# Edge sums of a graph stack: counted on VectorE in layer 2 instead of multiplied on TensorE in layer 1

## The chip, the cores and the metric

The kernel runs on one core of one Trainium2 chip. The core has five engines that run side by side, each with its own queue of instructions that it takes strictly in order: TensorE (PE in the profile; its weight loads are listed as PEld), VectorE (DVE), ScalarE (ACT), GpSimd (POOL) and SyncE (SP). Sixteen DMA engines move data; transfers are issued from the queues of SP, ACT and POOL. Engines wait for each other and for transfers by semaphores. The metric is the time of one execution on the device in microseconds.

## The reference, cut to what matters

A 4096 x 256 matrix `x` passes through four layers that share one 4096 x 4096 adjacency matrix `adj` of zeros and ones. Each layer adds its input and normalizes its rows.

```python
# layer 0
deg = sum(adj, axis=1); agg = adj @ x / max(deg, 1)
x = layernorm(x + relu(concat([x, agg]) @ W + b))
# layer 1, two steps; R = (adj + I) with rows scaled to sum 1
for n in range(2):
    A = top_p_attention(Xa, W1, W2, W3)     # softmax, the largest up to mass 0.9
    Xf = R @ Xf
    Xa = A @ Xa
    Z = Z + Xf @ U1[n].T + Xa @ U2[n].T
x = layernorm(x + layernorm(X + Z) * ln_g + ln_b)
# layer 2
neighbor_edge = einsum('ij,ji->i', adj, adj)[:, None]
x = layernorm(x + concat([x, adj @ x, neighbor_edge]) @ weight + bias)
# layer 3
x = layernorm(x + relu(normalized(adj + I) @ x @ W + b))
```

The change concerns `neighbor_edge`, the edge sum: for node i the number of nodes j with both `adj[i, j]` and `adj[j, i]` set. It is one number per row and is used in layer 2 alone. In the kernel it is the array `nef`, one column per tile of 128 rows.

## The kernel before, in words

**Tiles.** N = 4096 rows make 32 tiles of 128 (P). `adj` comes in twice as blocks of 128 x 128: `adjt` holds the transposed blocks of a row of tiles, `adjn` the blocks that stand opposite them. Both are f32 in memory; a transfer from POOL's queue turns them into 8-bit floats (F8) on the way in. Matrix products with `adj` use the 8-bit block, widened by ScalarE, as weights, and a right side of 512 columns: the upper bits of the operand and the rest (`split`, `load_halves`), so that two passes give f32 precision.

**Layer 0** (`l0_main`, up to about 350 us): for each tile `adjt` is loaded as `a8`, written back to memory as 8-bit `adj8_d`, widened in four pieces and multiplied. `column_counts` (L287) finds the row degrees on VectorE: the bytes of `a8` are added in pairs as 16-bit numbers, halving the width each time, with one shift to keep the bytes from running over; one 16-bit TensorE product with a column of ones adds the 128 partitions (`l0_degrees`, L304).

**Layer 1** (`run_step`, L941) is two steps over 32 tiles in a software pipeline. For index i it makes the logits of tile i + 2 (`logits_chunk`), searches the largest of tile i + 1 (`peak_groups`, `exp_rows`, `tops`, `pick`), and multiplies tile i (`pieces`, L720), in eight groups g. In step 0 a tile keeps 16 entries a row: POOL gathers the 16 sets of rows from memory (`gather`, L666, eight slots `G`), VectorE makes diagonal weights `dg`, TensorE multiplies (L758). Rows that need more are put off: `flag` (L579) counts them with two products of one column (L589, L590: `ones_sq`, `before`) and a scatter from POOL writes them to a list in memory (L603).

Beside this runs R @ Xf, one tile per index (`neighbours`, L674): SP loads two groups of 8-bit blocks from `adj8_d` (L678), ScalarE widens them (L680), TensorE multiplies (L683), `r_end` (L700) scales and stores. In step 0 alone the same blocks, still 8-bit, are multiplied with those of `adjn` (L693) into a bank `nef_ps`; `r_end` takes its diagonal on VectorE (L707) as the edge sum. The blocks of `adjn` are loaded from POOL's queue (L689) as halves of a tile, 256 KB each after conversion, into two buffers `b8`. While the edge products use the PSUM bank `nef`, the products of R use `acc` alone; from the end of step 0 on (`nef_done`) they take both in turn.

**Layer 2** (from about 2723 to 3002 us) and **layer 3** (to 3238 us): `piece` (L1102) loads a quarter of a tile's 8-bit blocks on SP and widens it on ScalarE, `main` multiplies 32 blocks into one of two banks, `l2_end` (L1126) adds the residual (`xi`), the bias, the part made ahead (`u`, from `zu_d`) and `w2e_sb * nef`, and normalizes; its power of -1/2 (L197) is POOL's. `l2_y` (L1144) makes layer 3's operand. Layer 2 begins after a loop that every engine enters together (`left_over`, L921), by loading the first pieces and the right side `zh` from `zu_d` (L1110).

**What sets the order.** The program text gives data dependences and a priority; a scheduler lays each engine's instructions out in one fixed order when the kernel is built, by costs and due times of its own. A buffer of a pool is used again when its last reader is done; that wait stands in the queue of whoever writes the buffer next, and what follows in that queue waits behind it.

Of the kernel before, what the change touches and what calls it, by code (L numbers as in the profile page):

```python
# [54 lines left out]
def gnn_stack(ctx, tc, x, adjt, adjn, w0, b0, w1, w2t, w3t, u1t, u2t, ln_g, ln_b, w2, b2, w3, b3, out):  # L55
# [44 lines left out]
    nc.vector.memset(ones_col, 1.0)  # L100
    mhalf = const.tile([P, 1], F32, name="mhalf")
# [18 lines left out]
    adj8_d = [dram.tile([P, NT, P], F8, name=f"adj8_{it}_d") for it in range(NT)]  # L120
    h_d = dram.tile([N + P, D], F32, name="h_d")
# [97 lines left out]

    with tc.tile_pool(name="l0", bufs=1) as l0, tc.tile_pool(name="l0w", bufs=2) as l0w:  # L220
# [28 lines left out]
        ones_bf = l0.tile([P, 1], BF16, name="ones_bf")  # L249
        nc.vector.memset(ones_bf, 1.0)  # L250
# [20 lines left out]
        def l0_main(it):  # L271
            acc = ps_acc.tile([P, 512], F32, tag=("acc", "nef")[it % 2], name="acc")

            a8 = l0.tile([P, NT, P], F8, tag="in", name="a8", bufs=SLOTS_IN)
            for s in (slice(0, NT // 2), slice(NT // 2, NT)):
                nc.gpsimd.dma_start(a8[:, s, :], adjt[it, :, s, :])
                nc.sync.dma_start(adj8_d[it][:, s, :], a8[:, s, :])

            def piece(it, c):
                a = l0w.tile([P, JP, P], F32R, tag="adjt", name="a", bufs=4)  # L280
                nc.scalar.copy(a, a8[:, c * JP : (c + 1) * JP, :])
                return a

            adj_matmul(l0w, acc, it, lambda jt: y0h[:, jt, :], piece)
            return acc, column_counts(a8)

        def column_counts(a8):  # L287

            pairs = a8.bitcast(U16).rearrange("p j i -> p (j i)")
            W = NT * P // 4  # L290
            s = l0w.tile([P, W], U16, tag="sums", name="sums", bufs=1)
            nc.vector.tensor_add(s, pairs[:, :W], pairs[:, W:])
            W //= 2
            nc.vector.tensor_add(s[:, :W], s[:, :W], s[:, W : 2 * W])
            words = s[:, :W].bitcast(I32)
            nc.vector.tensor_scalar(words, words, 3, None, op0=ALU.logical_shift_right)
            while W > P // 2:
                W //= 2
                nc.vector.tensor_add(s[:, :W], s[:, :W], s[:, W : 2 * W])
            counts = l0w.tile([P, P], BF16, tag="counts", name="counts")  # L300
            nc.vector.tensor_copy(counts, s[:, :W].bitcast(U8))
            return counts
# [49 lines left out]
    with tc.tile_pool(name="l1", bufs=1, reuse_waits="tile") as l1:  # L352

        cur = {"late": False, "n": 0, "nef_done": False}
# [4 lines left out]
        ones_sq = l1.tile([P, P], F32, name="ones_sq")  # L359
        nc.vector.memset(ones_sq, 1.0)  # L360

        before = l1.tile([P, P], F32, name="before")
# [216 lines left out]
        def flag(st):  # L579
# [9 lines left out]
            nc.tensor.matmul(pb[:, 0:1], ones_sq, st["bad"], start=True, stop=True)  # L589
            nc.tensor.matmul(pb[:, 1:2], before, st["bad"], start=True, stop=True)  # L590
# [83 lines left out]
        def neighbours(n, i, g, acc_r, pn, xf):  # L674

            if g % 2 == 0:
                cur["a8"] = cur["w"].tile([P, 2 * GP, P], F8, tag="adj8", name="adj8", bufs=3)
                nc.sync.dma_start(cur["a8"], adj8_d[i][:, g * GP : (g + 2) * GP, :])  # L678
            a = cur["w"].tile([P, GP, P], F32R, tag="adjq", name="adjq", bufs=2)
            nc.scalar.copy(a, cur["a8"][:, g % 2 * GP : (g % 2 + 1) * GP, :])  # L680
            for j in range(GP):
                jt = g * GP + j
                nc.tensor.matmul(acc_r, a[:, j, :], xf[:, jt, :], start=(jt == 0), stop=False)  # L683
            if g + 1 == NLC:
                nc.tensor.matmul(acc_r, ident_r, xf[:, i, :], start=False, stop=True)
            if pn is not None:
                if g % (NLC // 2) == 0:
                    cur["b8"] = cur["w"].tile([P, NT // 2, P], F8, tag="adjn8", name="adjn8", bufs=2)
                    nc.gpsimd.dma_start(cur["b8"], adjn[i, :, g * GP : g * GP + NT // 2, :])  # L689
                k = g % (NLC // 2) * GP  # L690
                for j in range(GP):
                    jt = g * GP + j
                    nc.tensor.matmul(pn[:, :P], cur["a8"][:, g % 2 * GP + j, :], cur["b8"][:, k + j, :], start=(jt == 0),  # L693
                                     stop=(jt == NT - 1))

        def r_acc(i):

            return ps_acc.tile([P, 512], F32, tag=("acc", "nef")[i % 2 if cur["nef_done"] else 0], name="acc_r", bufs=1)

        def r_end(i, acc_r, pn):  # L700
            xf_new = work.tile([P, D], F32, tag="xf_new", name="xf_new", bufs=1)
            nc.scalar.activation(xf_new, acc_r[:, :D], AF.Copy, scale=rs[:, i : i + 1])
            nc.vector.scalar_tensor_tensor(xf_new, acc_r[:, D:], rs[:, i : i + 1], xf_new, op0=ALU.mult, op1=ALU.add)
            if pn is not None:

                junk = spare_row.bitcast(F32)[:, :P]
                nc.vector.scalar_tensor_tensor(junk, pn[:, :P], 1.0, ident, op0=ALU.mult, op1=ALU.mult,  # L707
                                               accum_out=nef[:, i : i + 1])
            nc.sync.dma_start(rows(xf_d, i), xf_new)

        def r_product(n, i, xf):

            acc_r, pn = r_acc(i), None
            if n == 0:
                pn = ps_acc.tile([P, 512], F32, tag="nef", name="nef_ps", bufs=1)
            for g in range(NLC):
                neighbours(n, i, g, acc_r, pn, xf)
            r_end(i, acc_r, pn)

        def pieces(n, st, nxt, ops, rs_now=()):  # L720
# [10 lines left out]
            if with_r:  # L731
                i, = rs_now
                acc_r, pn = r_acc(i), None
                if n == 0:
                    pn = ps_acc.tile([P, 512], F32, tag="nef", name="nef_ps", bufs=1)
# [12 lines left out]
            for g in range(NLC):  # L748
# [19 lines left out]
                if with_r:  # L768
                    neighbours(n, i, g, acc_r, pn, cur["xf"])
# [11 lines left out]
            if with_r:  # L781
                r_end(i, acc_r, pn)
# [158 lines left out]
        def run_step(n, es):  # L941
# [99 lines left out]
            if n == 0:  # L1041
# [7 lines left out]
                cur["nef_done"] = True  # L1049
# [51 lines left out]
    with tc.tile_pool(name="l23", bufs=1, reuse_waits="tile") as l23:  # L1101
        def piece(it, c):  # L1102
            a8 = l23.tile([P, JP, P], F8, tag="a8", name="a8", bufs=5)
            nc.sync.dma_start(a8, adj8_d[it][:, c * JP : (c + 1) * JP, :])
            a = l23.tile([P, JP, P], F32R, tag="adjt", name="a", bufs=4)
# [3 lines left out]
        ahead = [piece(0, c) for c in range(NJP)]  # L1109
        zh = load_halves(l23.tile([P, 4 * J0 * D], F32, name="scratch"), zu_d[:N, :], nc.sync, slice(0, D))  # L1110
# [5 lines left out]
        yh = [pool.tile([P, NT // 2, 2 * D], F32R, tag="X", name=f"yh{k}") for k, pool in enumerate((xpool, l23))]  # L1116

# [3 lines left out]
        def main(it, halves):  # L1121
            acc = ps_acc.tile([P, 512], F32, tag=("acc", "nef")[it % 2], name="acc")
            adj_matmul(l23, acc, it, halves, lambda it, c: ahead.pop(0) if ahead else piece(it, c))
            return acc

        def l2_end(it, acc):  # L1126
# [7 lines left out]
            nc.vector.tensor_add(xi, xi, b2_sb)  # L1134
            nc.vector.tensor_add(u, u, xi)
# [34 lines left out]
        for it in range(NT):  # L1170
            acc = main(it, lambda jt: zh[:, jt, :])
# [54 lines left out]
```

## Time and profile before

| | us |
|---|---|
| median of 17 runs | 3248.4 |
| lowest and highest | 3228.41, 3255.78 |
| the profiled execution, its own time | 3253.88 |
| its span, first to last instruction | 3252.2 |
| layer 0 and first loads | 0 to about 350 |
| layer 1, step 0 | about 357 to 1250 |
| layer 1, step 1, put-off rows and zu | to about 2710 |
| layer 2 | 2723 to 3002 |
| layer 3 | 3002 to 3238 |

The profile is one execution. Its first part gives busy time by engine; the second cuts the span into 40 slices and shows the busy tenths of each; windows do the same for stretches that one names. Groups of instructions show line, engine, operation, `out<-in`, shapes and count, then the busy time, the mean time of one in ns, and how long the engine stood idle just before them, with what ended that. Successive TensorE instructions overlap, so their mean time is a latency; what one costs is the distance from start to start. Waits list who waited for whom: microseconds in total, times, and the longest.

### The profile page before, as it was taken

How to read it: one execution, taken by the hardware profiler on the slowest of the kernel's cores; microseconds unless marked ns; L12 is line 12 of the kernel's file. 1: busy time of each engine (PE TensorE's matmuls, PEld its weight loads, DVE VectorE, ACT ScalarE, POOL GpSimd, SP SyncE). 2: the span in 40 equal slices, each digit the busy share in tenths (PEclk: the TensorE clock that was granted, in tenths of full speed). 3: DMA queues.
4: the chain of work that ended last, by engine and by line, in shares of the span. 5: the costliest groups of instructions: out<-in, count | busy, mean ns of one | idle time of the engine just before them, and what ended most of it. 6: DMA issues, size and time to landing. Idle time of an engine off the chain costs nothing. (4 is left out here: it accounts for less than half of the span.)

```text
span 3252.2 us, 45754 instructions
## 1 busy us (share of the span) xinstructions
PE 2964.4 (91%) x14376; PEld 2339.7 (72%) x14376; DVE 2291.0 (70%) x7161; ACT 1746.2 (54%) x2906; POOL 789.2 (24%) x915
## 2 busy tenths in 40 slices
PE   7999889999999996799998999999999796999998
PEld 3788667777777774578877777877788554887886
DVE  4566778887787775268988896989799663444444
ACT  3555655665555553365545454645555334666664
POOL 1121256676666664000000001000100100000000
PEclk9999999999999997899999999999999898999999
DMA  9995468777777775230001110011011134333332
GB/s 171 162 174 115 83 117 137 141 141 139 138 139 139 137 135 129 90 91 20 23 25 25 33 38 27 28 35 38 24 36 28 61 127 132 107 110 102 104 109 81
DMA packets 247872, 300.14 MB, mean 92 GB/s; under 512 B 34688, under 2 KB 201536, under 8 KB 247616
## 3 DMA queue, kind: packets, MB, share of 16 engines
q0 software_dynamic: 46576, 104.94, 23.1%
q1 hardware_dynamic: 188800, 180.93, 18.5%
q10 hardware_dynamic: 12240, 11.23, 1.1%
q8 instruction: 116, 1.90, 0.3%
q14 instruction: 140, 1.15, 0.2%
HBM read 331.17 MB, written 66.45 MB: 122 GB/s over the span
## 5 line engine op out<-in xcount | busy, mean ns | idle before, releaser
L683 PE MATMUL acc_r<-xh,adjq 128*128 128x512 f32 x2048 | 610.7, 429 | 25.8 <-ACT adjq L680 14.9
L766 PE MATMUL acc_bank<-xa,at 128*128 128x256 f32 x2304 | 569.3, 388 | 29.9 <-ACT at L744 29.3
L669 POOL DMA_INDIRECT G<-x_d,cols x512 | 498.3, 973 | 290.6 <-PE acc_bank L758 177.6
L680 ACT CAST adjq<-adj 128x512 fp32r<-128x512 fp8e4 x512 | 316.4, 620 | 392.9 <-PE acc_r L683 309.6
L766 PEld LDWEIGHTS acc_bank<-xa,at 128*128 128x128 f32 x2304 | 424.6, 194 | 91.6 <-ACT at L744 40.5
L683 PEld LDWEIGHTS acc_r<-xh,adjq 128*128 128x128 f32 x2048 | 376.9, 191 | 122.0 <-ACT adjq L680 42.5
L197 POOL TENSOR_TENSOR rstd<-ve,mhalf 128x1 f32<-128x1 f32 x168 | 103.1, 614 | 1344.2 <-DVE ve L195 1289.9
L430 DVE MAX8 cand<-e 128x8 f32<-128x256 f32 x1024 | 383.1, 415 | 64.8 <-ACT e L412 63.5
L412 ACT COPY e<-lg 128x512 f32<-128x512 f32 x552 | 319.5, 585 | 196.9 <-PE lg L411 193.1
L411 PE MATMUL lg<-kS,q 128*128 128x512 f32 x1104 | 401.3, 449 | 4.8 <-ACT e L412 4.7
L758 PE MATMUL acc_bank<-G,dg 128*128 128x256 f32 x1024 | 291.5, 401 | 82.7 <-DMA G<-x_d,cols 72.7
L1106 ACT CAST a<-a 128x1024 fp32r<-128x1024 fp8e4 x256 | 267.9, 1048 | 158.7 <-PE acc L173 122.3
L758 PEld LDWEIGHTS acc_bank<-G,dg 128*128 128x128 f32 x1024 | 196.7, 198 | 140.2 <-DMA G<-x_d,cols 85.5
L527 DVE FIND_INDEX8 cols<-top,e 128x8 uint32<-128x4096 f32 x64 | 282.8, 4419 | 0.0
L173 PE MATMUL acc<-xh,a 128*128 128x512 f32 x1024 | 256.3, 403 | 22.3 <-DMA x2i<-x_d 17.8
L173 PE MATMUL acc<-y0h,a 128*128 128x512 f32 x1024 | 253.5, 400 | 0.0
L173 PEld LDWEIGHTS acc<-xh,a 128*128 128x128 f32 x1024 | 191.5, 190 | 66.4 <-ACT xh L149 24.5
L173 PE MATMUL acc<-yh,a 128*128 128x512 f32 x1024 | 233.7, 390 | 0.0
L744 ACT COPY at<-at_ps 128x512 f32<-128x512 f32 x296 | 173.5, 588 | 99.8 <-PE at_ps L741 98.1
L185 ACT COPY xt<-tr 128x256 f32<-128x256 f32 (+1 forms) x268 | 112.0, 425 | 212.9 <-PE tr L183 195.7
L173 PEld LDWEIGHTS acc<-yh,a 128*128 128x128 f32 x1024 | 192.1, 188 | 39.7
L173 PEld LDWEIGHTS acc<-y0h,a 128*128 128x128 f32 x1024 | 187.9, 188 | 42.2 <-issue 0.6
(287 smaller groups left out, 4598.9 us busy)
## 6 DMA issues: line engine op xcount, KB each, us to landing
adj<-adj_d SPq DMA_DIRECT2D x256, 128.0 KB
a<-adj_d SPq DMA_DIRECT2D x256, 128.0 KB
a<-in_adjt POOLq DMA_DIRECT2D x64, 256.0 KB
adj_d<-a SPq DMA_DIRECT2D x64, 256.0 KB
adjn<-in_adjn POOLq DMA_DIRECT2D x64, 256.0 KB
x_d<-x SPq DMA_DIRECT2D x64, 128.0 KB
xf_d<-xf_new SPq DMA_DIRECT2D x64, 128.0 KB
G<-x_d,cols POOLq DMA_INDIRECT x512
```

The costliest lines, as they stand in the source:

```text
L173: nc.tensor.matmul(acc, a[:, j, :], halves(jt), start=(jt == 0), stop=(jt == NT - 1))
L411: nc.tensor.matmul(pl[:, :LC], q[k], kS[:, s], start=(k == 0), stop=(k == 1))
L412: nc.scalar.copy(l[:, s], pl[:, :LC])
L430: nc.vector.max(dst[:, 8 * g : 8 * g + 8], src[:, g * GW : (g + 1) * GW])
L527: nc.vector.max_index(st["at"][:, 8 * r : 8 * r + 8], t8, st["e"][:, :N])
L669: nc.gpsimd.indirect_dma_start(out=g, out_offset=None, in_=x1_d, in_offset=bass.IndirectOffsetOnAxis(ap=st["at"][:, k : k + 1], axis=0))
L680: nc.scalar.copy(a, cur["a8"][:, g % 2 * GP : (g % 2 + 1) * GP, :])
L683: nc.tensor.matmul(acc_r, a[:, j, :], xf[:, jt, :], start=(jt == 0), stop=False)
L744: nc.scalar.copy(at[:, :G, :], ps[:, :G, :])
L758: nc.tensor.matmul(acc_a, dg[:, k % 4, :], st["G"][k], start=(k == 0), stop=(k == KEPT - 1))
L766: nc.tensor.matmul(acc_a, ats[g][:, j, :], cur["xa"][:, jt, :], start=(jt == 0), stop=(jt == NT - 1))
L1106: nc.scalar.copy(a, a8)
```

## The change: what it does

- In step 0 the edge products (L693) and their diagonal sums (L707) go. `neighbours` still loads the `adjn` blocks, and `keep_edges` writes each half from SP to a new tensor in memory, `adjn8_d`. A write is issued when the next half is asked for, so that it stands one half later in program order; `run_step` issues the last one. The products of R use the banks `acc` and `nef` in turn in both steps.
- In layer 2 `edge_row` loads a tile's 512 KB of `adjn8_d` on SP, two tiles ahead into two buffers. For each quarter, `both` takes on VectorE the bitwise and of the two 8-bit copies, as 32-bit words. `edge_count` runs `column_counts` on the result, adds the partitions with one TensorE product, and puts the number into `nef`.
- `column_counts` moves out of layer 0 and takes the pool as an argument; `ones_bf` becomes a constant of the whole kernel.
- Two additions of `l2_end` (`xi + b2`, `u + xi`) move from VectorE to GpSimd.
- `flag` copies `bad` to 16 bits; `ones_sq` and `before` are 16-bit too.
- The scratch of layer 2's start takes the memory of `yh`'s second half.

```diff
@@ neighbours, keep_edges, r_acc, r_end
-            if pn is not None:
-                if g % (NLC // 2) == 0:
-                    cur["b8"] = cur["w"].tile([P, NT // 2, P], F8, tag="adjn8", name="adjn8", bufs=2)
-                    nc.gpsimd.dma_start(cur["b8"], adjn[i, :, g * GP : g * GP + NT // 2, :])
-                k = g % (NLC // 2) * GP
-                for j in range(GP):
-                    jt = g * GP + j
-                    nc.tensor.matmul(pn[:, :P], cur["a8"][:, g % 2 * GP + j, :], cur["b8"][:, k + j, :], start=(jt == 0),
-                                     stop=(jt == NT - 1))
+            if edges and g % (NLC // 2) == 0:
+                half = slice(g * GP, g * GP + NT // 2)
+                t = cur["w"].tile([P, NT // 2, P], F8, tag="adjn8", name="adjn8", bufs=2)
+                nc.gpsimd.dma_start(t, adjn[i, :, half, :])
+                keep_edges(adjn8_d[i][:, half, :], t)
+
+        def keep_edges(dst=None, src=None):
+
+            if "edges" in cur:
+                nc.sync.dma_start(*cur.pop("edges"))
+            if dst is not None:
+                cur["edges"] = dst, src
...
-            return ps_acc.tile([P, 512], F32, tag=("acc", "nef")[i % 2 if cur["nef_done"] else 0], name="acc_r", bufs=1)
+            return ps_acc.tile([P, 512], F32, tag=("acc", "nef")[i % 2], name="acc_r", bufs=1)
...
-            if pn is not None:
-
-                junk = spare_row.bitcast(F32)[:, :P]
-                nc.vector.scalar_tensor_tensor(junk, pn[:, :P], 1.0, ident, op0=ALU.mult, op1=ALU.mult,
-                                               accum_out=nef[:, i : i + 1])
@@ flag
-            nc.tensor.matmul(pb[:, 0:1], ones_sq, st["bad"], start=True, stop=True)
-            nc.tensor.matmul(pb[:, 1:2], before, st["bad"], start=True, stop=True)
+            bad = small("bad16", 1, BF16)
+            nc.vector.tensor_copy(bad, st["bad"])
+            nc.tensor.matmul(pb[:, 0:1], ones_sq, bad, start=True, stop=True)
+            nc.tensor.matmul(pb[:, 1:2], before, bad, start=True, stop=True)
@@ layer 2
+        def edge_row(it):
+
+            b8 = l23.tile([P, NT, P], F8, tag="b8", name="b8", bufs=2)
+            nc.sync.dma_start(b8, adjn8_d[it])
+            return b8
+
+        def both(it, c, a8):
+
+            b = edge_rows[it][:, c * JP : (c + 1) * JP, :].bitcast(I32)
+            nc.vector.tensor_tensor(b, b, a8.bitcast(I32), op=ALU.bitwise_and)
+
+        def edge_count(it):
+
+            counts = column_counts(l23, edge_rows.pop(it))
+            ps = half("acc")
+            nc.tensor.matmul(ps[:, 0:1], counts, ones_bf, start=True, stop=True)
+            n = l23.tile([P, 1], I32, tag="edges", name="edges", bufs=2)
+            nc.vector.tensor_scalar(n, ps[:, 0:1], 1.0 / PER_ONE, None, op0=ALU.mult)
+            nc.vector.tensor_copy(nef[:, it : it + 1], n)
+
+        edge_rows = {0: edge_row(0), 1: edge_row(1)}
+        ahead = [piece(0, c, True) for c in range(NJP)]
+        zh = load_halves(l23.tile([P, NT * D], F32, tag="X", name="scratch"), zu_d[:N, :], nc.sync, slice(0, D))
...
-            nc.vector.tensor_add(xi, xi, b2_sb)
-            nc.vector.tensor_add(u, u, xi)
+            nc.gpsimd.tensor_add(xi, xi, b2_sb)
+            nc.gpsimd.tensor_add(u, u, xi)
...
-            acc = main(it, lambda jt: zh[:, jt, :])
+            acc = main(it, lambda jt: zh[:, jt, :], True)
+            edge_count(it)
+            if it + 2 < NT:
+                edge_rows[it + 2] = edge_row(it + 2)
```

## The prediction

> **What bounds the kernel now.** The page came first: TensorE (PE) is busy in 91% of the span, and its tenths stay at 9 nearly throughout, so a stage's length is PE's work plus the waits left in it. Second, the stages the change touches, by windows. Step 0 of layer 1 runs from about 357 to 1223 us, layer 2 from 2723 to 3002 us.
>
> ```profile
> PE 2964.4 (91%) x14376; PEld 2339.7 (72%) x14376; DVE 2291.0 (70%) x7161; ACT 1746.2 (54%) x2906; POOL 789.2 (24%) x915
> ...
> DMA  9995468777777775230001110011011134333332
> ```
>
> ```profile
> core 0: us, PE busy (x) PEld busy (x) DVE busy (x) ACT busy (x) POOL busy (x), PEclk, DMA share, GB/s
> ...
> 490.00:1222.00 732.00, 678.12 (x3739) 538.00 (x3738) 588.56 (x1737) 432.25 (x834) 486.32 (x512) 0.98 0.77 138
> ...
> 2755.00:3000.00 245.00, 245.00 (x1092) 197.10 (x1092) 106.29 (x316) 158.94 (x231) 15.91 (x29) 1.00 0.35 108
> ```
>
> ```profile
> 357.00:592.00 235.00, 10.98 (x19) 0.94 0.72 126
> 592.00:1223.00 631.00, 27.26 (x45) 0.98 0.77 138
> ```
>
> The last two rows are the edge blocks' loads alone (adjn, 64 of them): 19 are issued before 592 us and 45 after, spread evenly, while the 16 DMA engines are busy 72% and 77% of the time. So step 0 has a second resource that is nearly as full as PE. Layer 2 is PE's alone: 245 of 245 us.
>
> Third, who waits in step 0. PE waits for one thing only, gathered rows, and POOL, which issues the gathers, waits for PE to free their eight slots:
>
> ```profile
> PE acc_bank L758 <- DMA G<-x_d,cols: 53.9, 39, 3.4
> ```
>
> ```profile
> POOL G L669 <- PE acc_bank L758: 138.6, 156, 4.0
> ```
>
> Products end at 489.2 us (tile 4) and 1222.8 (tile 31) by the identity product that closes each: 733.6 us for 27, a period of 27.17 us. The window's 732 us are 26.94 such periods: PE 25.17 us a tile and 2.0 us of waits.
>
> **1. Products gone from step 0.** Per tile 32 8-bit matmuls and weight loads go.
>
> ```profile
> L693 PE MATMUL nef_ps<-adjn,adj 128*128 128x128 fp8e4 x1024 | 102.1, 223 | 5.1 <-DMA adj<-adj_d 3.0 <-DMA adjn<-in_adjn 2.0
> L590 PE MATMUL mm_bank<-bad,before 128*128 128x1 f32 x128 | 23.6, 254 | 0.0
> L589 PE MATMUL mm_bank<-bad,ones_sq 128*128 128x1 f32 x128 | 21.9, 240 | 26.3 <-DVE bad L561 26.2
> ```
>
> 223 ns is latency. Four in a row hold PE for 0.23 us (618.00 to the next start at 618.23 in the order of time), and over the window their start-to-start sum is 47.8 us: 1.77 us a tile. VectorE (DVE) loses its diagonal sum, 0.28 and 0.08 us. **Put-off counts:** two f32 products of one column are four passes, 11.2 us over the window, 0.42 a tile; as two 16-bit ones I take 0.15 (the 16-bit count of layer 0 lets the next matmul start 0.03 us after it; bounds 0.06 and 0.42). DVE gains a 128x1 copy, about 0.15 us by its 128x1 neighbours. PE per step-0 tile: 25.17 - 1.77 - 0.27 = 23.1 us. In step 1 PE is busy 235 of 250 us, so 32 x 0.27 = 8 us is the most; the copy lengthens DVE's chain into those products, 32 x 0.15 = 5 us, at worst all lost. I take -5 (-8 to +5). Product and count banks alternate now, so a product no longer waits for its predecessor's last read; that is inside the 23.1.
>
> **2. Where the loads go.** Before, a load's buffer (two of them) came free when PE's edge products had read it, and that spread the loads out. Now it comes free when the write of the 8-bit copy has landed, and nothing of PE holds it. In the built order of instructions the loads have moved: before, 19 stand ahead of the eighth scatter of a put-off list (L603, tile 7, at 590 us); in the changed kernel all 64 do. The groups read 14, 6, 8, 6, 8, 7, 8, 7 loads per tile and then none. They stand in POOL's queue between the gathers, and a load that waits for its buffer holds every gather behind it. The 64 writes stand in SP's queue, each waiting for its load; behind them wait the 8-bit loads of the products, the stores of xf, h, k and xa.
>
> Pace by the buffers. Rows:
>
> ```profile
> 357.24 1.15 POOL L689 DMA_DIRECT2D adjn<-in_adjn  x2 [0.21 <-issue]
> ```
>
> ```profile
> 363.75 1.33 PE L693 MATMUL nef_ps<-adjn,adj 128*128 128x128 fp8e4 x16 [0.59 <-DMA adjn<-in_adjn]
> ```
>
> ```profile
> 2706.54 3.21 DMA zu_d<-e,to_l
> ```
>
> A load lands 6.5 us after its issue; SP issues a write of this size in 0.32 us; the nearest write (256 KB, 2 KB a row) lands in 3.2. Some 10.3 us with the semaphores, two buffers: 5.15 us a load, 64 loads 330 us, so the eighth scatter at 357 + 330 = 687 instead of 590: +97.
>
> Pace by the DMA engines. Busy before in 357:592: 0.72 x 235 = 169 us. The trace's packet records give a load 128 packets of 324 ns (median) to 440 ns (mean here) on 16 engines, 2.6 to 3.5 us, and a 2 KB store packet 84 ns, 0.67 us a write. 45 more loads 117 to 159, 64 writes 43: 329 to 371 us. Of the 169, 29 are gather packets that sit for microseconds behind a scatter and need not be engine work. Floor 300 to 371 us: scatter at 657 to 728, +67 to +138. The two estimates overlap; I take +105 (bounds +45, were writes and half of a load's latency overlapped, and +160, 6.2 us a load, were both queues to add their waits).
>
> The Trainium skill speaks against hoping that writes on SP's queue pass beside POOL's loads: "DMA: Bandwidth & Descriptors", section "Issuing engines are not separate DMA queues", says that all issuers' transfers interleave on the same 16 engines. The 72% share here is that common pool; by the rule the sum of both stands, and without it the writes' 43 us would drop out.
>
> **3. Step 0 afterwards.** From there no load is left. Remaining: (1223 - 590) / 27.17 = 23.3 tiles. PE needs 23.1 us; DVE 21.8 - 0.36 + 0.15 = 21.6; POOL 16 gathers at 1.25 us (616.02 to 617.30 apart) and a scatter at 1.6, 21.6. Three engines within 7%: I take 24.2 (23.2 if PE alone, 25.5 if the waits stay as they are). 23.3 x 2.97 = -69 us (-92 to -39).
>
> **4. Layer 2.** Period 8.53 us, PE without a wait. PE adds a weight load and a one-column product, 0.03 to 0.17 us: I take 0.1, +3 us. DVE adds per tile four ands of 128x256 words (0.42 each by the f32 add of that shape; 0.29 by the single-input and), 1.68, and the count:
>
> ```profile
> L292 DVE TENSOR_TENSOR sums<-a x32: 681/687/694, 25.9 to 324.8; 128x1024 uint16<-128x1024 uint16 x32
> L294 DVE TENSOR_TENSOR sums<-sums x32: 405/409/418, 27.0 to 325.5; 128x512 uint16<-128x512 uint16 x32
> L296 DVE TENSOR_SCALAR sums<-sums x32: 283/287/292, 28.0 to 327.8; 128x256 int32<-128x256 int32 x32
> L301 DVE CAST counts<-sums x32: 216/217/321, 30.0 to 332.8; 128x128 bf16<-128x128 uint8 x32
> ```
>
> with three shorter adds (0.28, 0.22, 0.19): 2.29, and 0.31 for two 128x1 steps. Two adds of 0.42 move to POOL. DVE: 106.29 / 28.7 tiles = 3.70 + 4.28 - 0.85 = 7.1 of 8.6 us: hidden, with 1.5 us over. That slack is the cover, for counts feed a PE product, whose result DVE needs before the next tile: one ring through both in-order queues. POOL is busy 16 of 245 us. Two adds of unknown price there (0.29 by its 128x128 select; several us by its slow 128x32 power at the other end) go into a chain with a tile's slack; I take nothing. The Trainium skill speaks against that move: "GPSIMD Engine Reference", section 4.1 "Engine selection", keeps two-input elementwise work on VectorE, GpSimd being about twice as slow. An estimate by it is 1.7 us a tile, still under the row's idle time; no run here shows it. A 512 KB read more per tile meets a DMA share of 35%. The constant moved out of layer 0, the wider scratch and the earlier yh issue no instruction that wasn't there: nothing.
>
> **Start of layer 2.** Two edge rows (1 MB) stand ahead of the first pieces and of zu on SP, and the first ands and part of a count ahead of the first split on DVE. The zu stream already paces PE from 2714 to 2746 us. 1 MB at the 132 GB/s of this slice of the page is 8 us, part of it before anything could start; splits (8 x 1.9), 12 ands and three counts are 27 us of DVE against 24 us of stream. +6 (0 to +12).
>
> **Sum:** +105 - 69 - 5 + 3 + 6 = +40 us. The profiled execution took 3253.9 us (span 3252.2, 1.7 outside), 5.5 above the median of 17: 3294 by it, 3288 by the median. I say 3290.
>
> **The rivals.**
> - *The loads keep pace, step 0 gains.* If transfers overlap so that a load costs 4.4 us, the scatter comes at 639 (+49), and with PE alone afterwards (-92) the sum is -39: about 3210. For: the 27.17 us period had only 2.0 us of waits, so a stretch with DMA to spare costs little. Against: 72% of DMA time was taken before 45 loads came in. It decides below a pace of about 4.9 us a load (357 + 64 x 4.9 = 671, +81, less 81 with a 23.7 us period).
> - *Layer 2 becomes VectorE's.* If ands, counts and the ring take 9.6 us a tile, +32: about 3322. For: each count waits for four ands and a transfer. Against: 7.1 of 8.6.
> - *Both queues block each other.* SP waits for loads, POOL for writes, PE for both: 7 us a load, scatter at 805, +215 in place of 105: about 3400.
> - *Cancellation* within 0.2% (7 us, about what a measurement here can tell from no change).
>
> **How the numbers follow.** Forecast 0.60 (3255 to 3345, by its own bounds), rival one 0.16, layer 2 0.10, blocked queues 0.09, cancellation 0.05. Faster: rival one and a sliver of the forecast, 0.17; same 0.05; slower 0.78. The range goes from 3222, most of the way to rival one, to 3370, short of the blocked queues.
>
> **What would show it.** Right: all edge loads ahead of about 700 us; DMA share over 0.9 there, under 0.65 afterwards; in the first stretch PE waiting for G and adj, POOL's loads for writes; tiles of 35 to 40 us early and about 24 late; layer 2 at 8.6 us. Wrong: early tiles under 30 us, late ones still at 27, or PE waiting in layer 2 for counts.

## The result, and the profile after

The changed kernel takes 3345.3 us (median of 8 runs, 3343.1 to 3354.0), the one before 3248.0 beside it (47 runs): 1.031 times as long, interval 1.029 to 1.0324. Its profiled execution spans 3355.6 us, 103.4 more than before. The forecast was 3290.

The page of the changed kernel first: the total, the tenths of TensorE, and of the DMA engines.

```profile
PE 2908.7 (87%) x13256; PEld 2294.2 (68%) x13256; DVE 2377.4 (71%) x7513; ACT 1731.5 (52%) x2906; POOL 827.3 (25%) x979
...
PE   7999575657999998779998899989999796999998
...
DMA  9994688876566666331000211011011235544332
```

TensorE (PE) has 56 us less to do than before and is busy in 87% of the span where it was 91%. Its 9s break off at the fifth slice (about 340 us) and come back at the eleventh (840 us). That hole is where the loss arises. By windows (span, then busy time of PE, weight load, DVE, ACT, POOL; then granted clock, DMA share, GB/s):

```profile
455.00:747.00 292.00, 166.02 (x610) 125.89 (x611) 127.20 (x377) 93.34 (x180) 127.92 (x148) 0.75 0.82 142
...
812.00:1310.00 498.00, 472.55 (x2209) 387.85 (x2208) 453.71 (x1365) 328.16 (x651) 344.28 (x360) 0.98 0.65 137
2840.00:3101.00 261.00, 250.85 (x1115) 194.57 (x1114) 189.18 (x622) 152.49 (x228) 59.70 (x84) 1.00 0.50 154
```

In the first row PE works 57% of the time, and the DMA engines are at 0.82, not full. In the second the loads of `adjn` are over, and PE is as busy as ever at a DMA share of 0.65. The third is layer 2, where PE had worked 245 of 245 us and now misses 10 of 261.

Who waits, from 455 to 760 us (engine, tile, line, what it waited for; us in total, times, longest); SP's is the wait of the writes for their loads. Then the loads of `adjn` (L693) and their writes (L699) over the whole span:

```profile
POOL adjn L693 <- DMA adjn_d<-adjn: 135.6, 25, 13.1
PE acc_bank L756 <- DMA G<-x_d,cols: 115.6, 23, 17.8
```

```profile
SPq L699 <- DMA adjn<-in_adjn: 254.8, 44, 14.0
```

```profile
L693 POOL DMA_DIRECT2D adjn<-in_adjn x64: 527/572/632, 354.4 to 766.2; - x64
...
  DMA adjn_d<-adjn: 204.3, 35
...
DMA to landing us min/median/max: 5.1/7.3/11.2
```

```profile
DMA to landing us min/median/max: 2.0/3.0/10.2
```

The 64 loads run from 354 to 766 us, 6.5 us each. POOL stood 204 us before them, waiting for writes, with the gathers behind in its queue; PE waited for the gathered rows, up to 17.8 us at a time.

Stage by stage, from the two traces (us from the start of the span):

| | before | changed | difference so far |
|---|---|---|---|
| tile 7's count, ahead of its scatter | 589.7 | 747.2 | +157.5 |
| tile 31's last product of R | 1222.8 | 1310.2 | +87.4 |
| first product of layer 2 | 2723.5 | 2801.8 | +78.3 |
| end of layer 2's products | 3002.2 | 3101.6 | +99.4 |
| end of layer 3's products | 3238.6 | 3341.9 | +103.3 |

The scatter of tile 7 itself starts later than its count: at 592.2 us before and at 767.1 after, right behind the last load. By the count, it is +157 in the first eight tiles of step 0, -70 in the other 24, -9 in step 1, +21 in layer 2, +4 in layer 3.

### The profile page after: what moved, and what is told of

Its sections match the earlier page's. It is cut to its first block, busy times and chain, and to the rows that moved or that the text cites. A ratio compares the mean times of both kernels' runs of the same rounds, so it can differ in the third digit from the quotient of the medians.

```text
span 3355.6 us, 44016 instructions
## 1 busy us (share of the span) xinstructions
PE 2908.7 (87%) x13256; PEld 2294.2 (68%) x13256; DVE 2377.4 (71%) x7513; ACT 1731.5 (52%) x2906; POOL 827.3 (25%) x979
## 5 line engine op out<-in xcount | busy, mean ns | idle before, releaser
L687 PEld LDWEIGHTS acc_r<-xh,adjq 128*128 128x128 f32 x2048 | 384.7, 194 | 136.2 <-ACT adjq L684 59.9
L756 PE MATMUL acc_bank<-G,dg 128*128 128x256 f32 x1024 | 301.5, 421 | 179.8 <-DMA G<-x_d,cols 155.7
L756 PEld LDWEIGHTS acc_bank<-G,dg 128*128 128x128 f32 x1024 | 205.5, 208 | 242.1 <-issue 107.0
L1106 ACT CAST a<-a 128x1024 fp32r<-128x1024 fp8e4 x256 | 262.4, 1046 | 112.0 <-PE acc L176 78.3
L176 PE MATMUL acc<-xh,a 128*128 128x512 f32 x1024 | 261.3, 407 | 26.6 <-DVE xh L153 23.7
L413 PEld LDWEIGHTS lg<-kS,q 128*128 128x128 f32 x1104 | 199.7, 197 | 68.9 <-ACT e L414 36.9
```

Of the source, the lines that this page charges most:

```text
L176: nc.tensor.matmul(acc, a[:, j, :], halves(jt), start=(jt == 0), stop=(jt == NT - 1))
L413: nc.tensor.matmul(pl[:, :LC], q[k], kS[:, s], start=(k == 0), stop=(k == 1))
L756: nc.tensor.matmul(acc_a, dg[:, k % 4, :], st["G"][k], start=(k == 0), stop=(k == KEPT - 1))
L1106: nc.scalar.copy(a, a8)
```

## The experiments

They stood in five sets, each on one chip with the kernel before timed beside it: 3282.2, 3291.6, 3282.8, 3258.7 and 3220.3 us. Ratios are to that. (The record gives the first and the fifth set the same chip number, so the number alone does not explain these differences.) In all profiles of the second and third set, and in no other, ScalarE, VectorE and GpSimd have waits in step 0 that are put down to no instruction of this core, such as this one (the kernel with spread copies, 500 to 700 us):

```profile
ACT adjq L684 <- remote: 17.7, 6, 6.0
```

With them nearly the same order of instructions closes step 0 later, and roughly the more the larger their sum over these three engines: by 32 us in the kernel before (49 us of such waits), 45 with two pacing products (40), 77 in the changed kernel (64), 90 and 121 in the two kernels with spread copies (98 and 129). So the two sets serve for pairs within them and for later stages; the fourth set repeats what they left open.

Theory 1 was the forecast's: the crowding of the loads is the loss. Rivals: the amount of transfers, whatever their order, and layer 2.

### First set: order or amount

*Paced loads.* In each of a tile's eight groups a product of one column reads the group's last block of `adjn`, so that TensorE holds the buffer to the end of the half again:

```diff
+                cur["b8"] = t
+            if edges:
+                k = g % (NLC // 2) * GP + GP - 1
+                pn = half_bank("mm")
+                nc.tensor.matmul(pn[:, 0:1], cur["a8"][:, g % 2 * GP + GP - 1, :], cur["b8"][:, k, 0:1], start=True, stop=True)
```

> The changed kernel with the order of the loads held back: in each half of a tile one product of a single column on TensorE reads the half's last block of adjn, so that a load's buffer comes free no sooner than before the change; writes, layer 2 and all else stay as changed. Theory 1, order: what was lost in step 0 is the crowding of the 64 loads ahead of the put-off scatter of tile 7. Then that scatter comes at about 566 us (589.7 before, less 8 tiles by 3.0 us) instead of 747, tile 31's last product of R at about 1130 (1222.8 less 31 by 3.0) instead of 1310, and the time is 3248 - 93 - 9 + 21 + 4 = about 3170 us (3155 to 3190). Theory 2, amount: the DMA engines can't carry the 16.8 MB of writes beside the loads and gathers, in whatever order. Then the first tiles get better but all tiles stand near 27 us with PE waiting for G, and the time is 3250 to 3300. Theory 3, layer 2: the additional work there is the loss; nothing changes, 3345.

Measured: 3271.7 us, ratio 0.9976 (0.9956 to 0.9997). Tile 7's count is at 613.8 us, tile 31's last product at 1217.8. The crowd is gone (19 loads stand ahead of tile 7's scatter, as before the change), but so is the gain of 93 us: neither theory 1 nor layer 2 as the sole loss.

*No writes, loads crowded.*

```diff
-                keep_edges(adjn8_d[i][:, half, :], t)
...
-                keep_edges()
...
-            nc.sync.dma_start(b8, adjn8_d[it])
+            nc.sync.dma_start(b8, adj8_d[it])
```

> The changed kernel without the writes of adjn8_d; the loads of adjn stay, and layer 2 reads adj8_d in their place, so the edge sums are other numbers (the computation is changed in this one part). The loads still crowd ahead of tile 7's scatter, but a buffer comes free when its load has landed. If the pace of 6.4 us a load came from the two queues waiting for each other (a load for a write's landing, a write for a load's), the pace falls to about 4.7 us, the scatter comes at 354 + 64 x 4.7 = about 655 us, the late tiles stay at 23.7, and the time is about 3255 (3235 to 3270). If it came from what the DMA engines carry, the writes being a fifth of the bytes, the pace is about 5.5, the scatter near 705 and the time near 3300.

Measured: 3319.0 us, ratio 1.0104 (1.0064 to 1.0143). The loads' line of this kernel:

```profile
L693 POOL DMA_DIRECT2D adjn<-in_adjn x64: 527/542/902, 354.1 to 620.4; - x64
...
  DMA adjn<-in_adjn: 148.5, 48
```

64 loads in 266 us, 4.2 us each for 6.5 with writes. So a third of the pace goes with the writes and POOL's waits for them. Without them the loads fill the DMA engines (0.94 from 357 to 625 us), and all 64 now stand ahead of the fifth scatter. The time fits neither number: I had let the scatter of tile 7 follow the 64th load, and nearly four tiles at 25 us came in between (its count is at 712.5 us).

*No loads, no writes.* The block with the load in `neighbours` and the writes are left out, layer 2 reads as above.

> The changed kernel with neither loads nor writes of adjn in layer 1; layer 2 reads adj8_d in place of adjn8_d, so the edge sums are other numbers (the computation is changed in this one part), while the work of layer 2 is the same. Theory 1, order: step 0 is then as with paced loads, 23.5 to 24.2 us a tile, the scatter of tile 7 at 555 to 570 us, and the time is within 15 us of the kernel with paced loads, 3150 to 3175. Theory 2, amount: this kernel alone is fast, and the one with paced loads is 50 us or more behind it.

Measured: 3164.4 us, ratio 0.9638 (0.9601 to 0.9675); tile 31 closes at 1133.3, at 23.3 us a tile late in the step (tiles 18 to 29). The kernel with paced loads is 107 us behind it: amount, not order alone.

*Copies in step 1*, from memory to memory, held back by a small write:

```diff
-    neighbours(n, i, g, acc_r, n == 0, xf)
+    neighbours(n, i, g, acc_r, n == 1, xf)
...
-                t = cur["w"].tile([P, NT // 2, P], F8, tag="adjn8", name="adjn8", bufs=2)
-                nc.gpsimd.dma_start(t, adjn[i, :, half, :])
-                keep_edges(adjn8_d[i][:, half, :], t)
+                nc.sync.dma_start(adjn8_d[i][:, g * GP, :], cur["a8"][:, 0, :])
+                nc.gpsimd.dma_start(adjn8_d[i][:, half, :], adjn[i, :, half, :])
```

> The changed kernel with the copies of adjn moved to step 1, where the DMA engines are busy for 0.13 of the time: one transfer for each half goes from memory to memory and becomes 8-bit on the way; ahead of it a 16 KB write of a block that R's product has just loaded goes to the same place, so that the transfer waits for it and keeps pace with R's tiles. Theory 1: step 0 is as without any loads (tile 7's scatter at 555 to 570 us, tile 31's last product near 1120), step 1 hides the transfers, and the time is 3150 to 3175 us. Rival: 16 transfers stand at the head of step 1, where 11 tiles of R are made in a row; at 6 us each they hold back R's own loads there, up to 60 us: 3175 to 3230. Theory 3, layer 2: 3345.

Measured: 3193.8 us, ratio 0.9742 (0.9701 to 0.9784): faster than both kernels. Tile 31 closes at 1128.1, as without loads; the medians of this kernel and of the one without loads are 29 us apart, their traces 17, and 13 of these arise at the head of step 1, as the rival had it in kind.

### Second set: which part of the paced loads costs

*Both kernels again.*

> The kernel before, unchanged, profiled beside the experiments, so that stages are compared on one chip. The runs of it that stood beside the first four experiments took 3282 us, 1% more than the 3248 of the runs shown at first. Expected: layers 0, 2 and 3 and step 1 as before (layer 3 236 to 240 us), and the 34 us more in step 0, where transfers are nearest to a bound: tile 31's last product of R near 1250 us instead of 1222.8.

> The changed kernel, unchanged, on the same chip as the experiments. If its loss is the same share here, 3282 x 1.0307 = 3383 us; the scatter of tile 7 near 750 us or later.

Measured: 3290.7 and 3440.2 us, the latter 1.0465 (1.043 to 1.050). Before, tile 31 closes at 1255.0 us; layers 0, 2 and 3 and step 1 are within 6 us of the first trace. Changed, the first eight tiles are the same (738.9), but the other 24 take 648 us, not 563; step 0 has 64 us of the unexplained waits here.

*Paced loads without writes* (the two edits above together).

> The kernel with paced loads, and without the writes of adjn8_d (layer 2 reads adj8_d in their place, so the edge sums are other numbers). With paced loads tile 31 closed at 1217.8 us, without any loads at 1133.3: 85 us apart. Theory A, the queue of SP: each write stood at the head of SP's queue until its load had landed (451.7 us of 700 in all), R's own 8-bit blocks came late behind it, and ScalarE waited 107 us for them. Then without the writes tile 31 closes at 1135 to 1160 and the time is 3170 to 3195. Theory B, amount: the DMA engines (0.92 busy) set the pace, and the writes are 1.3 of some 7 us of their time that a tile's loads and writes take. Then it closes at about 1200 and the time is about 3255.

Measured: 3291.9 us, ratio 0.9998 (0.9976 to 1.002); tile 31 closes at 1256.2. Leaving out the writes and SP's waits brings nowhere near the 85 us that theory A needs, as far as a set with the unexplained waits can tell; the pair of the third set says 14 us. Theory A falls.

*Copies in step 0 from memory to memory*, the edit of the copies in step 1 with `n == 0` kept.

> The changed kernel with the copies of adjn made in step 0 from memory to memory, 8-bit on the way, each held back by a 16 KB write of a block of R's tile to the same place, as in the kernel that does this in step 1 (3193.8 us). SP's queue never waits for a load of adjn; the adjacency is read as often as before, and written as often as in the changed kernel. Theory A, the queue of SP: tile 31 closes at 1135 to 1165 and the time is 3175 to 3205. Theory B, amount: as with paced loads, 1200 to 1220 and 3255 to 3275.

Measured: 3376.2 us, ratio 1.0247 (1.0212 to 1.0282), tile 31 at 1329.9; a miss for both. POOL's loads now stood for the small writes (56.1 us in 12 waits from 600 to 1100 us) with the gathers behind them, but that is too little to explain it, and this profile has the most unexplained waits of all. Left open.

### Third set: the pacing device, and better copies

*Two pacing products a tile instead of eight*, and the same without writes:

```diff
-            if edges:
-                k = g % (NLC // 2) * GP + GP - 1
+            if edges and g % (NLC // 2) == NLC // 2 - 1:
+                k = NT // 2 - 1
```

> The kernel with paced loads had eight one-column products a tile, and TensorE's busy time was 23.0 us a tile in the late part of step 0 against 22.0 without loads. Here there are two a tile, in the last group of each half alone. Theory C, the device: the added products are what ate the gain; six fewer take 0.75 us off a tile, some 23 us in all, and the ratio to before goes from 0.998 to about 0.990. Theory D, the loads: 64 loads that stand beside R's transfers and the gathers cost what the edge products cost before, whatever holds them back; the ratio stays at 0.995 to 1.002. If order alone were the loss, as the first theory had it, the ratio would be 0.976.

> The kernel above without the writes of adjn8_d (layer 2 reads adj8_d in their place, so the edge sums are other numbers): the pair, run on one chip, prices the writes at this pace. If the writes, or SP's waiting for them, matter, this is 30 us or more faster than the kernel with them; with theory D it is within 15 us of it.

Measured: 3304.1 us, 1.0072 (1.0046 to 1.0099), and 3290.2, 1.0015 (0.9991 to 1.0039). The ratio is no better than the 0.9976 of eight products, and on a chip without the unexplained waits it is 0.9973 (fourth set): fewer products bring nothing, as far as two chips can be compared, so the device was not what ate the gain. The writes cost 14 us at this pace.

*Copies spread over tiles 11 to 31 of step 1*, three a tile:

```diff
+            if edges and i >= NT // 3 + 1 and (g % 3 == 0 or i + 1 == NT and g + 1 == NLC):
+                q = cur["copies"] = cur.get("copies", -1) + 1
...
```

> The copies made in step 1 from memory to memory (3193.8 us, ratio 0.9742), but spread over R's tiles 11 to 31, three a tile, so that none stands at the head of the step, where 11 tiles of R are made in a row. Without any copies the ratio was 0.9638, 29 us better: 9 us of that lay at the head of the step, 9 in the rest of step 1 and after it. Expected: the 9 us at the head come back, ratio about 0.971. If the copies cost the same wherever they stand in step 1, 0.974.

*The same with a row of its own for VectorE in layer 2.*

```diff
-            if edges:
-                both(it, c, a8)
...
+            nc.sync.dma_start(c8, adj8_d[it])
+            b, c = b8.bitcast(I32), c8.bitcast(I32)
+            nc.vector.tensor_tensor(b, b, c, op=ALU.bitwise_and)
```

> The kernel above with layer 2 changed: VectorE's bitwise and takes one 512 KB load of the tile's own 8-bit row, made ahead, in place of the four quarters that R's product loads; VectorE then has one instruction for four and waits for no quarter. Theory: the 21 us that layer 2 lost came from VectorE's waits for these quarters (51.9 us in 43 waits for them), with layer norm and the next operand queued behind; then its tiles go from 8.6 to 10.4 us back to 8.6, and the ratio improves by 0.004 to 0.006 (13 to 18 us). Rival: VectorE's work as such, or the two additions on GpSimd; then nothing changes, or it gets worse by the 512 KB more that each tile loads.

Measured: 3293.0 us, 1.0017 (0.9993 to 1.0042), and 3293.3, 1.004 (1.0021 to 1.0058). Their step 0 has nearly the order of the kernel with copies in step 1, yet tile 31 closes at 1249.0 and 1218.6, with the set's waits. By stage, the spread copies give back 9 us at the head of step 1 (343.6 for 352.5 us from tile 31 to the twelfth closing product of step 1) and lose 12 later (1169.6 for 1157.7 to layer 2): no gain. Layer 2 takes 298.2 us with a row of its own, 299.2 without. That decides little, for VectorE now stood 61 us for the two rows (28.1, 27.1 and 6.1) where it had stood 51.1 for the quarters; the fifth set decides it.

### Fourth set: the same question on one chip without such waits

> The changed kernel again, as the base for the three beside it on this chip. Its ratio to before was 1.031 and 1.0465 on two chips. Expected between these.

> The kernel with neither loads nor writes of adjn in layer 1 (layer 2 reads adj8_d in their place, so the edge sums are other numbers), again: ratio 0.9638 on its first chip. Theory L, the loads: their presence in step 0 costs, whatever the chip, and this kernel is 2.5% or more ahead of the one with paced loads and 6% or more ahead of the changed one. Theory S, the chip: the first result was that chip's; here it is within 1.5% of the kernel with paced loads.

> The kernel with the copies of adjn made in step 1, from memory to memory, again: ratio 0.9742 on its first chip, 29 us behind the one without loads. Its order of step 0 is that of the kernel without loads, so tile 31 closes within 15 us of it here. Theory L: it is 2% or more faster than before on this chip too. Theory S: it is within 1% of before.

> The kernel with loads held back by two one-column products a tile, again: ratio 1.007 on its first chip, a chip with unexplained waits. Beside the changed kernel it prices the order of the loads: theory L says 70 to 110 us less than that (tile 7's scatter 120 to 140 us earlier), and 80 to 110 us more than without loads.

| | changed | two pacing products | copies in step 1 | no loads, no writes |
|---|---|---|---|---|
| time, us | 3359.6 | 3249.0 | 3183.2 | 3147.9 |
| ratio to before (3258.7) | 1.0326 | 0.9973 | 0.9772 | 0.9664 |
| interval | 1.0288 to 1.0365 | 0.9954 to 0.9992 | 0.9736 to 0.9809 | 0.9632 to 0.9696 |
| tile 7's count | 741.2 | 606.9 | 571.2 | 570.0 |
| tile 31's last product of R | 1309.0 | 1199.5 | 1122.3 | 1113.3 |
| layer 2's first product | 2804.5 | 2691.6 | 2625.4 | 2604.7 |

Theory L holds. The change is the sum of three: -111 us for products and loads both taken out of step 0 (and all else), +101 for loads and writes back at an even pace (two pacing products a tile and SP's waits among it), +111 for the crowding. The kernel before had its loads at this pace too, so the first two belong together: products out, with the loads kept in even order, bring 10 us (all else of the change included), and the crowding turns that into a loss. The second term shows in the stage as a whole; windows of the kernel with two pacing products, then of the one without loads:

```profile
560.00:1190.00 630.00, 558.32 (x2566) 446.11 (x2565) 520.95 (x1553) 377.14 (x748) 429.29 (x460) 0.96 0.88 165
```

```profile
560.00:1100.00 540.00, 508.29 (x2386) 415.74 (x2386) 494.99 (x1471) 357.40 (x708) 378.39 (x391) 0.99 0.67 138
```

The DMA share rises from 0.67 to 0.88, and PE falls from 94% to 89% busy and from 0.99 to 0.96 of the clock. With the loads, SP's queue stands for them most of the time, though taking the writes away brought little (14 us in the third set):

```profile
SPq L706 <- DMA adjn<-in_adjn: 469.1, 49, 14.6
```

In step 1 the engines have the room. From 1500 to 2000 us with the copies, and for the same stretch (1480 to 1980) without:

```profile
1500.00:2000.00 500.00, 460.02 (x2317) 378.71 (x2316) 431.45 (x1438) 267.84 (x443) 50.84 (x68) 0.97 0.25 39
```

```profile
1480.00:1980.00 500.00, 457.65 (x2297) 376.60 (x2296) 427.29 (x1425) 264.40 (x441) 40.57 (x50) 0.97 0.13 29
```

PE does as much in both; the copies double a share of 0.13. From tile 31's last product to layer 2 they cost 11.7 us (1503.1 for 1491.4).

### Fifth set: step 1 and layer 2

*32-bit counts, no edge work in layer 2*: the edit of `flag` undone, and

```diff
+        nc.vector.memset(nef, 0.0)
...
-            acc = main(it, lambda jt: zh[:, jt, :], True)
-            edge_count(it)
-            if it + 2 < NT:
-                edge_rows[it + 2] = edge_row(it + 2)
+            acc = main(it, lambda jt: zh[:, jt, :])
```

> The changed kernel with the put-off counts in 32 bit again and without any edge work in layer 2 (no loads of adjn8_d, no bitwise and, no counts; the edge sums are zeros). Each lies in its own stage. From tile 31's last product of R to the first product of layer 2 the changed kernel took 1491.6 us and the one before 1500.7: if the 16-bit operands gave the 9 us, this kernel takes 1498 to 1503; if banks or loads did, 1490 to 1494. From layer 2's first product to its last the changed kernel took 299.8 us and the one before 278.7: if the edge work is the loss, this kernel takes 278 to 283; if the additions on GpSimd or the later scratch are, 295 to 300.

*The additions back on VectorE*:

```diff
-            nc.gpsimd.tensor_add(xi, xi, b2_sb)
-            nc.gpsimd.tensor_add(u, u, xi)
+            nc.vector.tensor_add(xi, xi, b2_sb)
+            nc.vector.tensor_add(u, u, xi)
```

> The changed kernel with the two additions of layer 2's end back on VectorE, the edge work left in. VectorE was busy for 6.3 us of a tile's 8.65 to 9 us; the additions make it 7.1. If layer 2 loses by VectorE's own waits for the quarters it takes the and of, in which the additions would stand behind, layer 2 takes 300 to 312 us for 299.8. If GpSimd's additions (0.75 and 0.84 us each) are late or slow VectorE down, it takes 285 to 295. The rest of the kernel is unchanged: ratio 1.030 to 1.034 where the changed kernel has 1.031 to 1.033.

Measured: 3304.9 us, ratio 1.0274 (1.0237 to 1.0311), and 3311.9, 1.0282 (1.0247 to 1.0316). Step 1, from tile 31's last product to layer 2, takes 1486.1 us with 32-bit counts and 1483.5 with 16-bit ones, both below the two numbers expected (1498 to 1503, or 1490 to 1494). Layer 2's products take 278.1 us without edge work, 282.4 with edge work and additions on VectorE, 299.8 in the changed kernel: the edge work alone is near free (278.7 before), the additions alone are free, together they cost. From 2840 to 3050 us, the additions on VectorE and then on GpSimd (changed kernel):

```profile
2840.00:3050.00 210.00, 210.00 (x949) 165.56 (x948) 165.66 (x582) 133.99 (x194) 19.69 (x25) 1.00 0.53 163
```

```profile
2840.00:3050.00 210.00, 202.15 (x900) 156.74 (x898) 153.32 (x504) 122.63 (x185) 49.26 (x69) 1.00 0.51 158
```

VectorE does more and PE has no gap. Groups of VectorE in layer 2 (busy us, mean ns), additions on GpSimd (changed kernel, fourth set, 2840 to 3100 us), then on VectorE (2812 to 3055 us):

```profile
L1157 DVE SCALAR_TENSOR_TENSOR t<-w2e_sb,nef,agg 128x256 f32<-128x256 f32 x29 | 18.2, 627 | 0.0
L1149 DVE TENSOR_TENSOR agg<-agg,acc 128x256 f32<-128x256 f32 x29 | 12.0, 412 | 0.0
L237 DVE CAST counts<-sums 128x128 bf16<-128x128 uint8 x29 | 9.3, 320 | 1.0
L1158 DVE TENSOR_TENSOR t<-t,u 128x256 f32<-128x256 f32 x29 | 12.0, 414 | 0.0
```

```profile
L1157 DVE SCALAR_TENSOR_TENSOR t<-w2e_sb,nef,agg 128x256 f32<-128x256 f32 x28 | 13.4, 480 | 0.0
L1149 DVE TENSOR_TENSOR agg<-agg,acc 128x256 f32<-128x256 f32 x28 | 11.6, 415 | 1.3 <-ACT agg L1148 1.3
L237 DVE CAST counts<-sums 128x128 bf16<-128x128 uint8 x28 | 6.4, 227 | 1.0
```

The same instruction is slower in the mean because some of its instances meet an addition of GpSimd. One such meeting, and one that costs nothing, in the order of time (start, us):

```profile
2881.78 0.73 POOL L1154 TENSOR_TENSOR x2i<-x2i,b_sb 128x256 f32<-128x256 f32 x1 [2.22 <-DMA x2i<-x_d]
2881.83 0.96 DVE L1157 SCALAR_TENSOR_TENSOR t<-w2e_sb,nef,agg 128x256 f32<-128x256 f32 x1
...
2889.30 0.41 DVE L1149 TENSOR_TENSOR agg<-agg,acc 128x256 f32<-128x256 f32 x1
2889.52 0.74 POOL L1154 TENSOR_TENSOR x2i<-x2i,b_sb 128x256 f32<-128x256 f32 x1 [2.34 <-DMA x2i<-x_d]
```

From 2840 to 3100 us, sorted by whether an addition of GpSimd overlaps them in time, instances of L1157 beside one take 913 ns in the mean (10), the others 476 (19); the bitwise ands (L1118) 555 (24) and 413 (87). Summed over VectorE's instructions, each form by itself, the difference is 15.6 us in these 260 us, and 19.4 over the whole layer. L1149, whose second operand is in PSUM, takes 412 ns either way, but it began first in all 10 meetings, so GpSimd's side has to tell: its addition took 0.74 us beside L1149, as it mostly does, and 1.02 us beside the one L1157 that began first. That the additions come late is not the loss: VectorE had no idle time before L1158, which takes their result `u`.

The Trainium skill, "SBUF — State Buffer", section "SBUF: two separate sides", has a rule for it: VectorE and GpSimd share one pair of ports, held by one instruction at a time, and on VectorE's side operations with two SBUF inputs or in a fast mode take part. The rows agree: the operations with two SBUF inputs are slowed, and so is the cast (564 ns for 227), while the one with a PSUM operand and GpSimd's additions don't hinder each other.

## Why the prediction was wrong in size

Of the 63 us between the +40 of the sum and the +103 of the traces, step 2 carries 52 and layer 2 12.

**Step 2, where the loads go: right in kind, mis-sized.** The term was +105 (bounds +45 and +160). It measured +157.5 by tile 7's count, and +175 by its scatter, the mark that the forecast named (767.1 us for 592.2). All 64 loads came first, tiles 5 to 9 took 50.7, 50.3, 51.6, 51.7 and 44.0 us where I had said 35 to 40, and PE waited for gathers and POOL for writes, as listed. What failed is the pace by the buffers, 5.15 us a load: 10.3 us for one round of a buffer (load, issue, write, semaphores), and two buffers side by side. In the trace a round takes 13.1 us in the mean: 7.05 from a load's issue to its write's issue, where the sum had 6.5, and 6.06 from there to the next load into the same buffer, where it had under 4. SP's queue added nothing: of the 10 loads whose landing is on record, 9 had their write issued at once. The rest is on POOL's side. In 39 of 62 rounds POOL stood waiting for the write and issued the next load 5.5 us after the write's issue. In the other 23 it was still at what stands ahead of the load in its queue, 18 times a gather, and the load went out after 7.1 us without a wait; this time ahead of a load was not in the sum. Without the writes the pace is 4.2 us. So the signs of the rival of blocked queues came (from 455 to 760 us SP waits for loads 255 us, POOL for writes 136), at a pace of 6.5 us between my 5.15 and its 7. The DMA share of "over 0.9" was wrong as well: 0.82.

**Step 3, afterwards: right in the period.** Tiles 11 to 31 take 23.7 us each, forecast 24.2. That -70 by the count stands beside -69 is partly luck: tile 9, at 44.0 us, is in it, and by the scatter it is -87. The fourth set shows what the period rests on: without a load the whole of step 0 runs at 23.9 us a tile in the mean. With loads at the old pace, tiles 5 to 13 took 28 to 33 us, and the mean is 26.3, hardly under the old 27.2. The 2.0 us of waits a tile in the old profile did not mean that loads were cheap; PE's 25 us covered them. That I first expected 3170 us from paced loads is the same error once more.

**Step 1: the sign right, the reason not shown.** -9 between the traces, -5 forecast, but 32-bit counts are only 2.6 us slower than 16-bit ones on one chip, and step 1 differs by more than that between chips. Where the rest comes from stays open.

**Step 4, layer 2: the term that was costed at nothing.** Forecast +9 with the start, measured +21. With the additions on VectorE it would have been +3.7, and the period 8.64 us, 0.11 more than before, which is the 0.1 that I gave the count's product; of the 6 us for the start, the first three tiles show 3.7, and 0.5 with the additions on VectorE. VectorE's slack, which I took as the cover, did hold for the edge work alone. I looked for the price of the two additions in GpSimd's own time, where they are harmless (0.74 us each in the median; GpSimd stays idle 77%), and not in what they do to VectorE: that term stood at nothing, and it measured 17 us. The Trainium skill's rule on two-input work ("GPSIMD Engine Reference", section 4.1 "Engine selection"), which the prediction set against the move, is borne out in its factor (0.74 us for 0.42), but the factor isn't the loss. That the 17 us come through VectorE's blocked instructions is shown as far as the 15.6 to 19.4 us of its time; the way from there to PE, whose waits in layer 2 are for the transposed rows of `x3`, was not separated:

```profile
PE mm_bank L1168 <- ACT xt L188: 9.9, 9, 1.6
```

Rival two, layer 2 as VectorE's with 9.6 us a tile, comes near the 9.15 measured after the first three tiles, but not by its mechanism: ands, counts and the ring alone take 8.64.

**Layer 3** was not in the sum. Its code is unchanged, and its tiles take 7.38 us for 7.25. The kernel with 32-bit counts and no edge work has 7.25 again, so it goes with one of these two edits; with which, and how, is open.

**The loads keep pace**, the rival on the other side, fell with the first window.

## What to carry to other kernels

An instruction that is removed may have been what held a transfer back: ask what frees the buffer afterwards, read in the built order of each queue where the transfers then stand, and count what stands ahead of a transfer in its queue into the pace. A transfer that is hidden under a busy engine comes to light when that engine gets faster; here it belonged in the stage whose DMA share was 0.13: with the copies there the kernel is 2.3 to 2.6% faster than the one before. (The same copies in step 0 gave a ratio of 1.0247, in a set with the unexplained waits.) An engine with idle time is not free if it shares something with the engine that is relieved.

## What was not expected

- In the stretch in which PE starves, its granted clock is lower: 0.75 from 455 to 747 us, 0.98 from 812 to 1310. Whether that cost time of its own, where PE waited for gathers anyway, no run separates.
- On two of the chips step 0 has the waits that are put down to "remote", up to 9 us each, and with them the same order of step 0 closes at 1219 to 1249 us rather than 1113 to 1133. Layers 0, 2 and 3 don't change. Their cause wasn't found.
- The best kernel run leaves layer 2's additions on GpSimd. Copies in step 1 with the additions on VectorE weren't tried.
